# Another order of the work in the second layer of a four-layer graph network

## Chip, cores and metric

The kernel runs on one core of a Trainium2 chip. The metric is the device time of one execution in microseconds. Shares and durations below come from one further execution, recorded by the hardware profiler. Engine names are those of the profile: PE is the matmul engine, PEld its weight load, DVE the vector engine, ACT the scalar engine, POOL the GpSimd engine and SP the engine that issues most loads.

## What is computed

Input is `x`, 128 graphs of 64 nodes with 128 features, and `adj`, one 64 by 64 matrix of edge lengths for each graph. About a quarter of its entries are not zero. Four layers follow each other, each with a residual and a layernorm. Layers 0 and 1 are continuous-filter convolutions: every edge length is spread over Gaussians, two dense layers with a softplus make a filter of 128 numbers from it, and the filter weighs the neighbour's features. Layers 2 and 3 are graph convolutions with a normalised adjacency. Layer 1, with the constant log 2 left aside, and the chain of layers are:

```python
g  = jnp.exp(coeff * (e[:, :, :, None] - offsets) ** 2)
h  = ssp(jnp.einsum('bijg,fg->bijf', g, W1) + b1)
Wf = jnp.einsum('bijf,gf->bijg', h, W2) + b2
rf = jnp.einsum('bjd,fd->bjf', r, Wa)
y  = jnp.einsum('bjf,bijf->bif', rf, Wf * Am * Am)
y  = ssp(jnp.einsum('bif,df->bid', y, Wd1) + bd1)
y  = jnp.einsum('bid,ed->bie', y, Wd2) + bd2
...
x = _layernorm(x + _L1_gnn_ref(x, adj, adj, ...), axis=-1)
x = _layernorm(x + _L2_gnn_ref(x, adj, ...), axis=-1)
x = _layernorm(x + _L3_gnn_ref(x, adj, ...), axis=-1)
```

## The kernel before, in words

The kernel works only on the edges that are there. Two graphs form a pair; the 128 nodes of a pair are the 128 partitions. For each pair the edges are packed into slots, sorted so that all pairs of a set have the same number of slots, and the slots of a pair are cut into three chunks. There are 64 pairs and two filter layers, so the main loop of `sparse_stack` has 3 x 128 turns and two more; turn i works on pair n = i / 3 and chunk k = i mod 3. Turns with n from 64 on belong to layer 1.

A chunk goes through three turns. In its first turn `filter_in` (L1774) makes the first filter product px, and ACT takes the exponential and later the logarithm (`softplus`). In its second turn `gather` (L1800) makes pg, the neighbours' features by a product with a one-hot matrix, which ACT copies. In its third turn `filter_out` (L1788) makes the second filter product pw and `message` (L1814) on DVE adds the bias to pw and multiplies with the gathered features into m. px, pg and pw each have a single tile of two PSUM banks: the next px waits for the exponential, the next pg for the copy, and the next pw for the message. When a pair's third chunk is done, `slot_sums` (L1837, L1841) sums the messages of each node in eight pieces on DVE; the loop runs 1, 4 and 4 of these pieces in the turns k = 0, 1 and 2. With k = 0, DVE also makes the one-hot matrix of the pair (hot, L1762), and with k = 0 and 1 ACT makes the Gaussians of the next pair.

Beside this run three kinds of work on groups of pairs. All are Python generators that yield between two steps, and the function `slot` runs one step of a queue. A step that ends with products yields True, and what takes the result out of PSUM is issued in the next call of `slot`, whatever queue that is for. `node_before` (queue `befores`) transposes the features (xT) and makes the products y (L1453) that `gather` uses. `node_after` (queue `nodes`) makes the products u, o and back (L1565, L1584, L1593), adds the residual (ny, L1597) and normalises with `layernorm`. `graph_convs` (queues `convs`) makes layers 2 and 3 of the group: gx, gh, hw, nT, gh, hw, o, then a layernorm, then nT, sup, o, and a second layernorm, and hands the rows to `store_rows`, which scatters them to the output by DMAs that POOL issues. Convolutions of the groups follow in alternation in `convs[0]` and `convs[1]`. In `layernorm` the statistics are on DVE (L1415, L1416); for a group of four pairs the inverse root and the normalising of each pair are on POOL (L1422, L1423, L1428). `scaled` (L1630) puts the scaled adjacency into a block matrix on POOL.

Layer 1 begins with pair 8 and ends with pairs 0 to 7. It has groups of four pairs, and at its end groups of two, one and one, which have a queue of their own each in `last`. After the loop, all queues are drained in turn.

[...] a fixed order (`in_order`) is laid over all engines. So the order of the calls in the loop is the order of the products on PE. Before the change a turn's order on PE is px, pg, nodes, features (k = 1), the small groups, pw, convolutions.

## Time and profile before

| | |
|---|---|
| time, median of 3 runs | 1592.23 us (1591.06 to 1595.87) |
| profiled execution, time | 1607.39 us |
| profiled execution, span from first to last instruction | 1605.5 us |
| PE busy | 1432.6 us, 89% of the span |
| DVE, ACT, POOL busy | 1355.6, 1335.6, 732.5 us |
| share of PE in the chain that ended last | 45%, DVE 27%, ACT 10% |

The profiled execution is 15.2 us slower than the median. Layer 1 begins at about 760 us and its last pw starts at 1537.95 us. One group of four pairs takes twelve turns, for instance from 1235.60 to 1284.90 us. A line of the timeline has start, duration, engine, source line, operation, out<-in, shape and the number of equal instructions merged; in square brackets stands how long the engine had been idle and what released it. A line of the waits has the engine and what it wanted to do, whom it waited for, and then total, times and longest in us. The names of the products are those above; matmul rows count passes, so one product of two halves is x4.

### The profile page before, as it was taken

What the parts mean: (1) busy time and instruction counts of PE and PEld (TensorE: products, weight loads), DVE (VectorE), ACT (ScalarE), POOL (GpSimd) and SP (SyncE); (2) the same over time, 40 slices, a digit from 0 to 9 for tenths busy, and PEclk for the clock granted to TensorE, in tenths of its full rate; (3) what the DMA queues carried; (4) which work ended last, traced back from release to release, by engine and by line L of the source; (5) the groups of instructions that cost most, each with busy time, mean ns of one, the idle gap of its engine ahead of it and who ended that gap; (6) DMA issues with size and microseconds to landing.
All of it is one profiled execution on the core that took longest, in us unless ns stands there. A gap on an engine that the chain in (4) does not pass through costs nothing.

```text
span 1605.5 us, 24221 instructions
## 1 busy us (share of the span) xinstructions
PE 1432.6 (89%) x6813; PEld 802.6 (50%) x6813; DVE 1355.6 (84%) x3547; ACT 1335.6 (83%) x1847; POOL 732.5 (46%) x1174
## 2 busy tenths in 40 slices
PE   1276999999999999999999999999999999999974
PEld 1133454555554555555445555556555555555543
DVE  7687889999989999889878888888888888888873
ACT  1266898989888989889999998999989999899842
POOL 2425246555655644425611255433554435543454
PEclk9998999999999999999999999999999999999976
DMA  7654464645455544447555455544554455455200
GB/s 257 209 123 114 112 138 123 135 124 145 124 136 134 136 122 113 113 111 178 149 151 129 128 142 132 129 124 125 144 132 120 120 134 138 124 141 123 64 8 23
DMA packets 122289, 205.67 MB, mean 128 GB/s; under 512 B 47956, under 2 KB 80034, under 8 KB 121506
## 3 DMA queue, kind: packets, MB, share of 16 engines
q1 hardware_dynamic: 110784, 187.61, 46.7%
q0 software_dynamic: 6576, 14.99, 2.9%
q10 hardware_dynamic: 4786, 1.43, 0.4%
q8 instruction: 57, 0.93, 0.3%
q14 instruction: 86, 0.70, 0.2%
HBM read 185.29 MB, written 18.64 MB: 127 GB/s over the span
## 4 chain that ended last, share of the span: by engine, by line
PE 45%; DVE 27%; ACT 10%; DMA 7%; issue 6%; SPq 3%; POOL 2%; another core or an unknown queue 1%; ACTq 0%; DVEq 0%; POOLq 0%
PE pw L1788 16%; PE px L1774 9%; DVE m L1814 8%; PE pg L1800 7%; DVE agg L1837 6%; ACT h L951 4%; DVE hot L1762 2%; DVE at L1182 2%; PE hw L1673 2%; SPq L1299 2%; ACT g L951 2%; PE y L1453 2%; ACT d L951 1%; DVE st L1415 1%; PE o L1584 1%
## 5 line engine op out<-in xcount | busy, mean ns | idle before, releaser
L951 ACT ACTIVATE h<-h,half 128x672 f32<-128x672 f32 (+13 forms) x385 | 353.1, 917 | 0.1
L1837 DVE TENSOR_REDUCE agg<-m 128x16 f32<-128x240 f32 (+13 forms) x896 | 325.0, 411 | 3.0
L951 ACT ACTIVATE g<-pg 128x672 f32<-128x672 f32 (+12 forms) x384 | 303.2, 790 | 26.4 <-DVE m L1814 13.2
L1800 PE MATMUL pg<-hot,ys 64*128 64x336 f32 (+12 forms) x1536 | 308.8, 478 | 7.9 <-DVE hot L1762 7.0
L1788 PE MATMUL pw<-h,w_L_gnn_W2T 128*128 128x420 f32 (+5 forms) x768 | 301.9, 516 | 15.2 <-DVE m L1814 15.2
L1814 DVE SCALAR_TENSOR_TENSOR m<-pw,c_L_gnn_b,g 128x840 f32<-128x840 f32 (+5 forms) x192 | 200.9, 1046 | 115.6 <-PE pw L1788 88.0
L1788 PE MATMUL pw<-h,w_L_gnn_fw 128*128 128x336 f32 (+6 forms) x768 | 264.4, 467 | 28.3 <-DVE m L1814 22.0
L951 ACT ACTIVATE h<-px,c_L_gnn_b 128x840 f32<-128x840 f32 (+5 forms) x192 | 178.7, 931 | 53.6 <-PE px L1774 52.8
L1814 DVE SCALAR_TENSOR_TENSOR m<-pw,c_L_gnn_fb,g 128x672 f32<-128x672 f32 (+6 forms) x192 | 176.9, 921 | 50.0 <-PE pw L1788 31.2
L951 ACT ACTIVATE h<-px,c_L_gnn_fb 128x672 f32<-128x672 f32 (+6 forms) x192 | 159.3, 830 | 71.2 <-PE px L1774 46.4
L1788 PEld LDWEIGHTS pw<-h,w_L_gnn_W2T 128*128 128x128 f32 x768 | 132.5, 191 | 141.1 <-DVE m L1814 37.6
L1774 PE MATMUL px<-d,fw 64*128 64x336 f32 (+6 forms) x768 | 166.2, 507 | 40.8 <-DMA d<-d_dram 29.2
L1800 PEld LDWEIGHTS pg<-hot,ys 64*128 64x128 f32 x1536 | 146.3, 188 | 108.1 <-issue 17.5
L1788 PEld LDWEIGHTS pw<-h,w_L_gnn_fw 128*128 128x128 f32 x768 | 132.5, 191 | 120.6 <-DVE m L1814 62.2
L1762 DVE SCALAR_TENSOR_TENSOR hot<-j,row,w 128x1212 f32<-128x1212 bf16 (+12 forms) x128 | 177.0, 1383 | 9.0 <-issue 9.0
L1774 PE MATMUL px<-d,w1t 64*128 64x420 f32 (+5 forms) x768 | 181.1, 548 | 1.7 <-ACT h L951 1.6
L1422 POOL TENSOR_SCALAR rs<-mv 128x4 f32<-128x4 f32 x61 | 14.5, 237 | 344.0 <-DVE mv L1416 335.6
L1774 PEld LDWEIGHTS px<-d,fw 64*128 64x128 f32 x768 | 59.7, 188 | 132.2 <-ACT h L951 44.4
L951 ACT ACTIVATE d<-d,neg_off 128x1212 f32<-128x1212 f32 (+12 forms) x128 | 119.8, 936 | 7.1 <-issue 7.1
L1428 POOL TENSOR_SCALAR x_all<-ny,mv,rs 128x128 f32<-128x128 f32 x124 | 116.4, 947 | 3.3
L1030 POOL DMA_INDIRECT rows<-comb,goes x64 | 67.9, 1061 | 97.1 <-DMA rows<-comb,goes 69.6
L1774 PEld LDWEIGHTS px<-d,w1t 64*128 64x128 f32 x768 | 57.8, 184 | 66.8 <-ACT g L951 26.8
(264 smaller groups left out, 2209.6 us busy)
## 6 DMA issues: line engine op xcount, KB each, us to landing
d<-d_dram SPq DMA_DIRECT2D x32, 315.0 KB
w<-w_dram SPq DMA_DIRECT2D x32, 315.0 KB
d<-d_dram SPq DMA_DIRECT2D x32, 303.0 KB
w<-w_dram SPq DMA_DIRECT2D x32, 303.0 KB
w<-w_dram SPq DMA_DIRECT2D x32, 252.0 KB
j<-j_dram SPq DMA_DIRECT2D x32, 157.5 KB
j<-j_dram SPq DMA_DIRECT2D x32, 151.5 KB
d<-d_dram SPq DMA_DIRECT2D x16, 300.0 KB
```

Source lines behind the costliest of these rows:

```text
L951: latest = nc.scalar.activation(out_, in_, func, **kw)
L1030: nc.gpsimd.indirect_dma_start(out=into, out_offset=bass.IndirectOffsetOnAxis(ap=at, axis=0), in_=rows, in_offset=None,)
L1182: nc.vector.max_index(out=at[:, r, cut], in_max=top[:, r, cut], in_values=av[:, r, :])
L1299: (engine if name == "d" else nc.sync).dma_start(to, dram_ap(slots[layer, name][s], first, [[0, to.shape[0]], [1, n]]))
L1428: (nc.gpsimd if n == GS else nc.vector).tensor_scalar(dst[:, s, :], y[:, s, :], mv[:, s, 0:1], rstd[:, s : s + 1], ALU.subtract, ALU.mult,)
L1453: nc.tensor.matmul(ps[:, s, :], lhsT=xt[:, s * P : (s + 1) * P], rhs=w["win"], start=True, stop=True)
L1762: nc.vector.scalar_tensor_tensor(hots[n][:, 0:size], j[:, 0:size], near, wt[:, 0:size], ALU.is_equal, ALU.mult)
L1774: nc.tensor.matmul(ps[:, b, 0:n], lhsT=w1, rhs=d[rows, col : col + n], start=True, stop=True)
L1788: nc.tensor.matmul(c["pw"][:, b, :], lhsT=c["w"]["w2"], rhs=c["h"][:, b, :], start=True, stop=True)
L1800: nc.tensor.matmul(ps[:, b, 0:n], lhsT=y[rows, :], rhs=hots[c["n"]][rows, at], start=True, stop=True,)
L1814: nc.vector.scalar_tensor_tensor(messages[n][:, :, at], c["pw"], c["w"]["b2"], c["g"], ALU.add, ALU.mult)
L1837: nc.vector.tensor_reduce(av[:, :, :, r], both, AX.X, ALU.add)
```

## The change

Five edits, all of which act on layer 1 or on work that runs beside it.

1. In turns of layer 1, `filter_out` comes ahead of the small groups and the nodes' step. `message` stays behind them.
2. In turns of layer 1, the features' step runs with k = 0 instead of k = 1, right after `gather`.
3. `node_after` of layer 1 no longer yields once before u.
4. `graph_convs` of a group of four no longer waits two turns between the scaling and gx, and yields once more between sup and o.
5. The pieces of the sums run 2, 4 and 5 in the turns k = 0, 1 and 2 of layer 1.

```diff
         if layer == 0:
             yield from zero_share(q, agg)
-        elif q < len(GROUPS[1]) - 1:
-            yield
         u, _ = bank(f"u_{name}", n)
...
         if n == GS:
             scaled(2, q)
-            yield from wait_steps(2)
         flat, ps = bank(f"gx_{q}", n)
...
         y3 = yield from times("sup", lambda s: xs[:, s, :], lambda s: nT3[:, s, :])
+        if n == GS:
+            yield
         flat, ps = bank(f"o3_{q}", n)
...
-        run(sums, (1, 4, 4)[k])
+        run(sums, ((1, 4, 4), (2, 4, 5))[n >= NP][k])
...
         if c1 is not None:
             gather(c1)
+        if n >= NP and k == 0 and befores:
+            slot(befores)
         if c is not None:
             softplus(c)
             if k == 2 and sines:
 
                 sines.popleft()()
-        slot(nodes)
-        if k == 1 and befores:
-            slot(befores)
+        if n < NP:
+            slot(nodes)
+            if k == 1 and befores:
+                slot(befores)
+        if c2 is not None:
+            filter_out(c2)
         for queue in last.values():
             slot(queue)
+        if n >= NP:
+            slot(nodes)
         if c2 is not None:
-            filter_out(c2)
             message(c2)
         if convs[0]:
             slot(convs[0])
```

## Prediction

> **What bounds the kernel now.** I read the page's first part, then the busy table by stretches of time, then the waits of the matmul engine (PE) in layer 1, then one group of four pairs on each engine.

> ```profile
> PE 1432.6 (89%) x6813; PEld 802.6 (50%) x6813; DVE 1355.6 (84%) x3547; ACT 1335.6 (83%) x1847; POOL 732.5 (46%) x1174
> ```

> ```profile
> 850.00:1490.00 640.00, 621.21 (x3023) 356.24 (x3021) 535.49 (x1132) 590.00 (x748) 282.20 (x345) 1.00 0.52 131
> 1490.00:1606.00 116.00, 81.68 (x377) 53.39 (x376) 73.82 (x203) 59.01 (x116) 57.05 (x76) 0.82 0.09 24
> ```

> The columns of the second fence are stretch, length, busy PE, PEld, DVE, ACT, POOL, granted clock. The stretch 850 to 1490 is layer 1 with graph convolutions beside it: PE is busy 621.2 of 640 us, so an edit of order can win at most 18.8 us there. Then comes a tail of 116 us in which nothing is full. The waits of PE between 850 and 1490 say what the 18.8 us are:

> ```profile
> PE pw L1788 <- DVE m L1814: 15.2, 25, 1.1
> PE o L1584 <- ACT gy_hw L951: 1.6, 5, 0.3
> PE o L1726 <- ACT xt L951: 1.5, 1, 1.5
> PE px L1774 <- ACT h L951: 0.4, 1, 0.4
> ```

> 15.2 of 18.7 us are one wait: the second filter product pw (there is one pair of PSUM banks for it) cannot start before DVE's message m of the step before has read it. In the timeline it recurs in the same place of each group:

> ```profile
> 1273.61 1.56 PE L1788 MATMUL pw<-h,w_L_gnn_W2T 128*128 128x384 f32 x4
> 1275.09 0.92 PE L1774 MATMUL px<-d,w1t 64*128 64x384 f32 x4
> 1275.84 0.81 PE L1800 MATMUL pg<-hot,ys 64*128 64x384 f32 x4
> 1277.71 1.56 PE L1788 MATMUL pw<-h,w_L_gnn_W2T 128*128 128x384 f32 x4 [1.05 <-DVE m L1814]
> ```

> Between two pw stand only px and pg, 0.75 us each from start to start, and DVE has in that time the elu, reductions and layernorm statistics queued ahead of the message:

> ```profile
> 1274.03 0.74 DVE L1614 TENSOR_SCALAR er<-gh,c_L_gnn_b 128x512 f32<-128x512 f32 x1
> 1274.68 0.66 DVE L1837 TENSOR_REDUCE agg<-m 128x16 f32<-128x224 f32 x2
> 1275.26 0.67 DVE L1841 TENSOR_REDUCE agg<-m 128x8 f32<-128x256 f32 x2
> ...
> 1276.65 1.00 DVE L1814 SCALAR_TENSOR_TENSOR m<-pw,c_L_gnn_b,g 128x768 f32<-128x768 f32 x1
> ```

> So PE bounds layer 1, and its small bubbles come from uneven filling, not from a lack of DVE time: DVE is busy 535 of 640 us.

> [...] here the four normalising operations of one group take 3.1 us in some places and 3.87 us in others. I use that as the spread of their price.

> **Order of the products.** No arithmetic is added or removed, so I count what stands after each pw. For the group from 1235.60 to 1284.90 before: o; nothing; gx and y; gh and u; nT; sup; hw, o3 and o; nT and back; gh; nothing; nothing; hw and xT. In the changed program, same group: gx; gh; nT and y; sup; u and hw; nT and o3; gh; o; back; hw; o; xT. Three empty places become none, and the fullest holds two products instead of three. Prices from start to start in this group: pw 1.39 to 1.49, px and pg 1.50 together, a 128-column set of four 0.98, u or gh of 512 columns 0.96, a set of transposes 0.5. The sum over twelve steps is about 47.5 us in either order; before takes 49.30 with 1.66 idle. Placing a product after pw instead of before it moves 0.1 us (pw 1.39 against 1.29) from one to the other: cost nothing.

> **DVE in the new order.** Prices from start to start: message 0.95, hot 1.35, a reduction 0.38 (the last two 0.59), half the statistics of a layernorm 0.83, er, ny, gz, nT each 0.60, em with er 1.30. The sums' pace (2, 4, 5 in place of 1, 4, 4) costs no instruction: k=0 and k=2 steps get one reduction more, k=1 loses two. The heaviest stretch between two messages is the one after back: ny 0.6, er 0.6, two reductions 0.75, hot 1.35, statistics 0.83, message 0.95, together 5.1 us. A message ends at the earliest 2.6 us after its pw starts (1.5 + 0.1 + 1.0). 2.6 + 5.1 = 7.7 us stands against two PE periods of 3.9 = 7.8 us: no wait, but no room. All other stretches (2.1 to 4.9 us, against periods of 3.3 to 4.8) leave over 0.7 us. I take 0.3 us a group as what comes back, 0 to 0.7 as bounds; 13 groups: 4 us.

> **ACT.** Its heaviest step has h, g, softplus (2.3 us), u's three passes (1.9), the gaussian (1.05) and hw's copy (0.5), 5.7 us against a PE period of 4.8; the next ACT step has 2.9 against 4.5, and px needs only the exponential at its head. Cost nothing, hidden under pw and the step's two products; uncovered it would be 0.9 us a group.

> **Waiting turns removed.** Now gx follows back by four pw in place of seven: 15.0 us instead of 24.7. Between them lie the statistics and POOL's normalisation of x.

> ```profile
> 1280.16 0.23 POOL L1422 TENSOR_SCALAR rs<-mv 128x4 f32<-128x4 f32 x1 [0.74 <-DVE mv L1416]
> 1280.48 1.04 POOL L1423 TENSOR_TENSOR rs<-rs,neg_half 128x4 f32<-128x4 f32 x1
> 1281.62 3.87 POOL L1428 TENSOR_SCALAR x_all<-ny,mv,rs 128x128 f32<-128x128 f32 x4
> ```

> Before: back at 1268.84, x done at 1285.5, 16.7 us later, 8.0 us ahead of gx. After, ny is added one turn earlier, so x is due 13.2 to 13.8 us after back (7.7 to the last statistics, 0 to 0.6 behind a scatter and blocks, 5.5 on POOL): 1.2 to 1.8 us left. For sup the margin is thinner: POOL passes scatter, add, blocks, add, scatter (about 7.9 us with the waits for the scatter's DMA that the trace shows at 1.4 to 1.5 each), then 4.6 us of normalising: 26.0 us after back against sup at 26.6. When a scatter lands late (waits of up to 2.6 us are in the trace) PE stands at sup. Bounds 0 to 2 us a group, taken 0.4; 13 groups: 5 us. The bias add on xs and the scatters themselves are on POOL and are counted in this. SP's loads keep their order and turn. The features (xT, then y) go from the turn k=1 to k=0, one turn earlier; they are first gathered from in the next group, eight turns on, so nothing waits for them, and their copies on ACT (0.48 us each) are as many as before: cost nothing. Layer 0 keeps its order on all engines. The yield added after sup only places o3 one turn later, beside nT.

> **The tail.** After the last pw (1537.95) the end is 60 us away.

> ```profile
> 1547.51 1.06 PE L1685 MATMUL gx<-ident,x_all 128*128 128x128 f32 x4
> 1596.74 0.18 DVE L1416 BATCH_NORM_AGGREGATE mv<-st 128x2 f32<-128x6 f32 x1 [3.20 <-POOL gz L1428]
> ```

> This gx is that of the last convolution of four pairs; in the new order it stands ahead of the last pw, and 1.06 + 2.08 us of its products leave the stretch after u of the last pair. It also ends one turn earlier, so the last statistics need not wait 3.20 us for POOL's normalising of it. Against that, gx needs x (done at 1535.9), which can hold the last pw by 1 to 2 us, and the chain of the last pair keeps its turns. Gain between 0 and 6.3 us; I take 4.

> **Sum.** 18.7 - 4 - 5 + 4 = about 14 us, 15 with one px wait of 1.0 us at 818 that goes with the same spreading. The profiled execution would go from 1607.39 us (span 1605.5) to about 1592; its own 15 us over the median of 1592.23 is not part of this. Taken off the median: 1577.

> **Rivals.** All bubbles go and the tail gains in full: 18.7 + 6.3 = 25 us, 1567; for it speaks that no gap is empty; against it the 0.1 us of room after back. Half: the DVE wait reappears after back and hot at 0.7 us (9 us) with POOL's 5: 18.7 - 14 + 3 = 8 us, 1584. No difference: the tail is held by the last pair and the waits merely move; within 4 us of 1592. It would then not do what it says, though the order of the program is certain. Slower: POOL becomes the bound at sup and gx. From 1.75 us of wait a group on, (18.7 + 4) / 13, the change loses; with both scatter waits at 2.6 us and the normalising at 3.87, sup is late by about 2.6 us, which gives 13 x 2.6 - 22.7 = 11 us, 1603. For it speaks that POOL has waits on DMA in each group; against it, POOL is busy 282 of 640 us.

> **How the numbers follow.** Likeliest 1577 at 0.42, full 1567 at 0.20, half 1584 at 0.18, no difference 0.12, slower 0.08. Faster by over 0.3% (below 1587.5; about what a measurement of this kernel can tell from no change) is 0.80. The range 1566 to 1591 leaves out the slower case and the ends of the first and fourth.

> **What would show it.** Right: in the stretch of layer 1 PE's waits of pw for m fall from 15 us to under 5, the group's period is about 48 us, gx follows back by four pw, and the last wait of 3.2 us is gone. Wrong: PE waits for x_all of POOL at gx or sup by over 1 us a group, or the wait for m stays above 8 us, or the tail after the last pw stays at 60 us.

## Result and profile after

After 1580.67 us, median of 17 runs (1575.56 to 1590.36); before 1592.69 us, median of 17 runs (1589.88 to 1599.38). The ratio is 0.9915, 95% interval 0.990 to 0.993: the medians differ by 12.0 us, and the ratio alone gives 13.5, with 11 to 16 as its interval. The profiled execution after took 1590.36 us (span 1588.5); it is the slowest of the 17. That of before, with 1607.39 us, lies above all 17 of its runs too, so the traces are compared by stretches below.

First the profile's page, its busy times and the chain that ended last:

```profile
PE 1435.7 (90%) x6813; PEld 811.5 (51%) x6813; DVE 1358.1 (85%) x3547; ACT 1336.6 (84%) x1847; POOL 766.3 (48%) x1174
...
PE 34%; DVE 20%; DMA 14%; POOL 13%; ACT 9%; issue 6%; SPq 3%; ACTq 0%; DVEq 0%; POOLq 0%
```

The work is the same (equal counts of instructions). In the chain PE had 45% before, POOL 2% and DMA 7%; now POOL and DMA hold 27% together. The busy table by stretches:

```profile
850.00:1472.00 622.00, 614.00 (x2966) 357.48 (x2968) 527.10 (x1114) 575.80 (x729) 312.14 (x344) 0.99 0.51 131
1472.00:1589.00 117.00, 87.50 (x396) 56.47 (x394) 77.44 (x208) 65.90 (x123) 55.44 (x75) 0.82 0.13 34
```

PE's idle time in layer 1 fell from 18.8 us in 640 to 8.0 in 622. Its waits in that stretch are of another kind:

```profile
PE sup L1671 <- POOL x_all L1428: 5.6, 16, 0.8
PE gx L1682 <- POOL x_all L1428: 2.0, 3, 1.1
```

The wait of pw for DVE's message, 15.2 us before, is gone, and all that is left is a wait for POOL's normalising of x. In the group from xT at 1219.31 to xT at 1267.41 the period is 48.10 us, where it was 49.30.

I cut each execution in three: up to layer 1's first px (the first with `w1t`), from there to the start of the last pw (called layer 1 below), and the tail. Before: 745.00, 792.95, 67.55 us. After: 735.54, 788.22, 64.74 us. The first difference, 9.5 us, is no gain: nothing ahead of layer 1 was changed, and the profiled executions of all the kernels below begin layer 1 anywhere from 727.8 to 747.6 us. So this execution shows a gain of 7.5 us behind the start of layer 1; the other sixteen have no trace. What it lost lies in two groups, of 52.4 and 54.14 us. This is PE in the second:

```profile
1330.04 1.44 PE L1787 MATMUL pw<-h,w_L_gnn_W2T 128*128 128x380 f32 x4
1331.75 0.49 PE L1671 MATMUL sup<-nTs,x_all 128*128 128x128 f32 x2 [0.26 <-POOL x_all L1428]
1332.52 0.49 PE L1671 MATMUL sup<-nTs,x_all 128*128 128x128 f32 x2 [0.29 <-POOL x_all L1428]
1333.84 0.49 PE L1671 MATMUL sup<-nTs,x_all 128*128 128x128 f32 x2 [0.82 <-POOL x_all L1428]
1334.61 0.49 PE L1671 MATMUL sup<-nTs,x_all 128*128 128x128 f32 x2 [0.29 <-POOL x_all L1428]
1335.03 1.28 PE L1773 MATMUL px<-d,w1t 64*128 64x380 f32 x4
1336.09 1.48 PE L1799 MATMUL pg<-hot,ys 64*128 64x380 f32 x4
1337.51 2.19 PE L1787 MATMUL pw<-h,w_L_gnn_W2T 128*128 128x380 f32 x4
```

```profile
1325.00:1330.00 5.00, 5.00 (x30) 2.94 (x27) 5.00 (x12) 4.83 (x7) 4.39 (x6) 1.00 0.47 130
1330.00:1335.00 5.00, 3.34 (x14) 1.81 (x13) 3.21 (x5) 2.73 (x4) 4.56 (x4) 1.00 0.47 127
1335.00:1340.00 5.00, 5.00 (x15) 2.44 (x15) 0.19 (x1) 3.11 (x4) 0.00 (x0) 0.66 0.22 52
```

sup takes each pair of x as POOL finishes it, 0.49 us of work each 0.77 us or more. Right after it the granted clock (the share of PE's full clock that the chip allowed) is 0.66 over five microseconds, that is 3.4 us at half speed, and px, pg and pw take 1.28, 1.48 and 2.19 us where they took 0.91, 0.81 and 1.44 just before. PE had been busy for 2.01 us of the 3.41 ahead (last section). So PE lost more here than the length of the waits, but not behind all waits: three of 1.32 us in all at 1431 to 1433 were followed by a granted clock of 1.00.

### The profile page after: what moved, and what is told of

It is laid out like the page before. It is cut to its first block, busy times and chain, and to the rows that moved or that the text cites. A ratio compares the mean times of both kernels' runs of the same rounds, so it can differ in the third digit from the quotient of the medians.

```text
span 1588.5 us, 24203 instructions
## 1 busy us (share of the span) xinstructions
PE 1435.7 (90%) x6813; PEld 811.5 (51%) x6813; DVE 1358.1 (85%) x3547; ACT 1336.6 (84%) x1847; POOL 766.3 (48%) x1174
## 4 chain that ended last, share of the span: by engine, by line
PE 34%; DVE 20%; DMA 14%; POOL 13%; ACT 9%; issue 6%; SPq 3%; ACTq 0%; DVEq 0%; POOLq 0%
PE pw L1787 12%; PE px L1773 7%; PE pg L1799 5%; DVE m L1813 5%; POOL x_all L1428 5%; DMA out_dram<-gz,at_row 4%; ACT h L951 4%; DVE agg L1836 3%; DMA d<-d_dram 2%; DVE hot L1761 2%; POOL rs L1423 2%; SPq L1299 2%; POOL gz L1428 2%; DMA w<-w_dram 2%; ACT g L951 2%
## 5 line engine op out<-in xcount | busy, mean ns | idle before, releaser
L951 ACT ACTIVATE h<-h,half 128x672 f32<-128x672 f32 (+13 forms) x385 | 353.6, 918 | 0.1
L951 ACT ACTIVATE g<-pg 128x672 f32<-128x672 f32 (+12 forms) x384 | 303.4, 790 | 30.2 <-DVE m L1813 18.3
L1836 DVE TENSOR_REDUCE agg<-m 128x16 f32<-128x240 f32 (+13 forms) x896 | 319.5, 411 | 2.9
L1787 PE MATMUL pw<-h,w_L_gnn_W2T 128*128 128x420 f32 (+5 forms) x768 | 306.9, 522 | 1.3 <-DVE m L1813 1.2
L951 ACT ACTIVATE h<-px,c_L_gnn_fb 128x672 f32<-128x672 f32 (+6 forms) x192 | 159.3, 830 | 55.9 <-PE px L1773 55.6
L951 ACT ACTIVATE h<-px,c_L_gnn_b 128x840 f32<-128x840 f32 (+5 forms) x192 | 178.7, 931 | 27.0 <-PE px L1773 26.3
L1422 POOL TENSOR_SCALAR rs<-mv 128x4 f32<-128x4 f32 x61 | 14.7, 241 | 310.5 <-DVE mv L1416 308.5
L951 ACT ACTIVATE d<-d,neg_off 128x1212 f32<-128x1212 f32 (+12 forms) x128 | 120.3, 940 | 6.7 <-DMA d<-d_dram 6.7
L1030 POOL DMA_INDIRECT rows<-comb,goes x64 | 70.8, 1106 | 94.6 <-DMA rows<-comb,goes 60.4
L1428 POOL TENSOR_SCALAR x_all<-ny,mv,rs 128x128 f32<-128x128 f32 x124 | 106.2, 864 | 3.3
```

Source lines behind the costliest of these rows:

```text
L951: latest = nc.scalar.activation(out_, in_, func, **kw)
L1030: nc.gpsimd.indirect_dma_start(out=into, out_offset=bass.IndirectOffsetOnAxis(ap=at, axis=0), in_=rows, in_offset=None,)
L1422: nc.gpsimd.tensor_scalar(rstd, mv[:, :, 1], LN_EPS, None, ALU.add)
L1428: (nc.gpsimd if n == GS else nc.vector).tensor_scalar(dst[:, s, :], y[:, s, :], mv[:, s, 0:1], rstd[:, s : s + 1], ALU.subtract, ALU.mult,)
L1787: nc.tensor.matmul(c["pw"][:, b, :], lhsT=c["w"]["w2"], rhs=c["h"][:, b, :], start=True, stop=True)
L1836: nc.vector.tensor_reduce(av[:, :, :, r], both, AX.X, ALU.add)
```

## Experiments

My theory was that places between two pw that hold no other product make the wait for the message, and that filling them removes it. The rivals: DVE's backlog of reductions makes it; and POOL, pressed by the removed turns, is the next bound. "Layer 1" is the length defined above, of the profiled execution; 792.95 us before, 788.2 after. The waits of PE are those from 850 us on.

### Each edit alone

Edit 1 alone (`filter_out` ahead of the nodes' step):

```diff
-        slot(nodes)
+        if n < NP:
+            slot(nodes)
...
+        if c2 is not None:
+            filter_out(c2)
         for queue in last.values():
             slot(queue)
+        if n >= NP:
+            slot(nodes)
         if c2 is not None:
-            filter_out(c2)
             message(c2)
```

> The kernel before with edit 1 alone: pw ahead of the nodes' step in layer 1. Theory of the filled places (the gain is that no two pw of layer 1 stand without a product between them while DVE is behind): this order still has two empty places next to each other in each group, so PE's wait for m stays at 10 to 15 us between 850 us and the end of layer 1, and the time is within 4 us of 1592.7. Rival, pw early (the gain is that pw starts earlier): most of it shows here, about 1582 us.

Edit 2 alone (the features' step with k = 0):

```diff
+        if n >= NP and k == 0 and befores:
+            slot(befores)
...
-        if k == 1 and befores:
+        if n < NP and k == 1 and befores:
             slot(befores)
```

> The kernel before with edit 2 alone: xT and y with k = 0 instead of k = 1. The order of the products has one empty place in a group instead of three. Theory of the filled places: PE's wait for m falls by about half, 1585 to 1588 us. Rival, pw early: no change, within 3 us of 1592.7.

Edits 3 and 4 alone (the turns of waiting):

```diff
-        elif q < len(GROUPS[1]) - 1:
-            yield
...
-            yield from wait_steps(2)
...
+        if n == GS:
+            yield
```

> The kernel before with edits 3 and 4 alone: no waiting turns in the nodes and convolutions, one turn between sup and o. Two empty places in a group, not next to each other. Theory of the filled places: wait for m about half, and the tail about 3 us shorter: 1583 to 1588 us; PE may wait for POOL's x_all at gx or sup by 1 to 3 us in all. Rival, the tail alone is the gain: 1588 us with the wait for m unchanged at 15 us.

Edit 5 alone (the pace of the sums):

```diff
-        run(sums, (1, 4, 4)[k])
+        run(sums, ((1, 4, 4), (2, 4, 5))[n >= NP][k])
```

> The kernel before with edit 5 alone: the sums run 2, 4, 5 instead of 1, 4, 4. Order on PE as before. Theory of the filled places: within 3 us of 1592.7, wait for m 12 to 17 us. Rival, the gain is an even load of DVE: 1583 us with the wait for m under 7 us.

| alone | us (median) | ratio to before, 95% | layer 1 | PE waits in layer 1 |
|---|---|---|---|---|
| edit 1 | 1589.83 | 0.9987 (0.9972 to 1.0002) | 789.3 | pw for m 8.5, o for ACT's copy of sup 3.5 |
| edit 2 | 1589.39 | 0.9979 (0.9966 to 0.9991) | 787.6 | pw for m 11.9 |
| edits 3 and 4 | 1652.04 | 1.0368 (1.0342 to 1.0395) | 852.8 | below |
| edit 5 | 1593.85 | 1.0009 (0.9998 to 1.0021) | 792.4 | pw for m 15.3 |

The medians of edits 1 and 2 are 2 to 3 us lower, but the interval of edit 1 includes no change; edit 5 wins nothing. With edit 2 the wait for m fell by a fifth, where I had expected half, and with edit 1 it fell below the 10 to 15 us that I had expected. Edits 3 and 4 alone lose 59 us, where I had expected a gain. Their waits of PE:

```profile
PE gx L1682 <- POOL x_all L1428: 22.4, 32, 1.4
PE sup L1671 <- POOL x_all L1428: 17.0, 30, 2.5
```

The wait for m is gone there too, but 39.4 us of waiting for POOL came instead, and 44.4 us of layer 1 run at half clock (before: 3.4 us, at its very end); the mean granted clock of the whole execution is 0.970, before 0.982. PE idles 25.7 us more than before in layer 1 and is busy for 34.1 us longer. Of the latter the half clock is at most 20.5 us by estimate, half of the 41.0 us that it lasts longer; the other 13.6 may be gx and sup, which come there in single pieces; that was not tried. So the rival "POOL becomes the bound" is real.

### Which half needs which

The changed kernel with the turns of waiting put back, that is edits 1, 2 and 5:

```diff
+        elif q < len(GROUPS[1]) - 1:
+            yield
...
+            yield from wait_steps(2)
...
-        if n == GS:
-            yield
```

> The changed kernel with the turns of waiting back (edits 1, 2 and 5 alone). Theory of filled places: one place between two pw stays empty in a group, and POOL has its room, so no wait of PE for x_all and no half-clock stretch; some 5 us of pw waiting for m stay: 1580 to 1586. Theory that the removed turns are what hurts (as in the run with edits 3 and 4 alone, +59 us): without them the time is below that of the changed kernel, 1572 to 1578. Rival: that edits 1 and 2 together already fill what matters and the turns are free in this company: the time of the changed kernel, within 3 us.

1630.17 us, ratio 1.0238 (1.0209 to 1.0268), layer 1 821.4 us. All three expectations failed. pw waits 0.2 us for m, so edits 1 and 2 do fill the places; but sup waits 19.5 us in 41 pieces for POOL. Neither half of the change is of use alone, and both lose to the same engine. POOL in that kernel, one group:

```profile
1279.98 1.58 POOL L1449 TENSOR_TENSOR x_all<-x_all,b_L_gnn_bd 128x512 f32<-128x512 f32 x1 [1.44 <-PE xT L1444]
...
1287.41 1.10 POOL L1030 DMA_INDIRECT out_dram<-gz,at_row  x1 [0.18 <-issue]
1288.54 0.62 POOL L1630 TENSOR_TENSOR blocks<-a_all,dinv 64x256 f32<-64x256 f32 x1
1292.29 2.61 POOL L1630 TENSOR_TENSOR blocks<-a_all,dinv 64x256 f32<-64x256 f32 x3 [3.13 <-DMA out_dram<-gz,at_row]
1295.18 1.00 POOL L1030 DMA_INDIRECT out_dram<-gz,at_row  x1 [0.28 <-POOL blocks L1630]
1300.23 0.96 POOL L1030 DMA_INDIRECT out_dram<-gz,at_row  x1 [4.05 <-DMA out_dram<-gz,at_row]
```

In this trace the second block scaling behind a scatter, or the next scatter, waits until it has landed: 4.9 us from 1287.41 to 1292.29, 5.05 from 1295.18 to 1300.23. After, the same stretch is:

```profile
1268.76 2.08 POOL L1030 DMA_INDIRECT out_dram<-gz,at_row  x1 [0.18 <-issue]
1270.88 1.28 POOL L1449 TENSOR_TENSOR x_all<-x_all,b_L_gnn_bd 128x512 f32<-128x512 f32 x1
1272.10 0.62 POOL L1628 TENSOR_TENSOR blocks<-a_all,dinv 64x256 f32<-64x256 f32 x1
1273.19 0.61 POOL L1628 TENSOR_TENSOR blocks<-a_all,dinv 64x256 f32<-64x256 f32 x1 [0.47 <-DMA out_dram<-gz,at_row]
1273.88 1.28 POOL L1686 TENSOR_TENSOR x_all<-x_all,b_L_gnn_b 128x512 f32<-128x512 f32 x1
...
1277.85 4.00 POOL L1428 TENSOR_SCALAR x_all<-gz,mv,rs 128x128 f32<-128x128 f32 x4
```

The add L1449 (1.28 us) stands between a scatter and what waits for it, and the wait is 0.47 us. That gave a new theory: what makes x late is how the scatters lie in POOL's queue.

### Is DVE the cause of the old wait, and is the pace needed

The kernel before with layer 1's sums over two slots instead of all for seven of eight residues; it leaves out part of the messages:

```diff
-            one = v[:, :, base[r] : base[r] + caps[r]]
+            one = v[:, :, base[r] : base[r] + (2 if layer == 1 else caps[r])]
```

> The kernel before with layer 1's sums of messages taken over two slots instead of all for seven of eight residues: it leaves out part of the messages, so that DVE's reductions are shorter and their number the same. Theory that PE's waits of pw for m come from empty places in PE's own order (a wait of the length of the message's chain minus the work between): the waits fall in part, as far as reductions stand ahead of the message, to some 8 to 12 us, time 1580 to 1588. Rival, they come from DVE's backlog of reductions: the waits fall below 4 us and the time to 1576 to 1580.

1580.14 us, ratio 0.9909 (0.9887 to 0.9931), layer 1 778.5 us. The wait of pw for m:

```profile
PE pw L1788 <- DVE m L1814: 4.5, 11, 0.5
```

That is nearer to the rival. DVE's reductions ahead of the message make it late: with shorter ones, in PE's old order, 10.7 of the 15.2 us go. Filled places give DVE time, shorter reductions need less.

The changed kernel with the pace of before, `run(sums, (1, 4, 4)[k])`:

> The changed kernel with the sums' old pace (1, 4, 4) in layer 1. Theory that the pace is of no weight, as alone: within 2 us of the changed kernel. Rival, the pace is needed in the new order (four reductions ahead of the message in the turn k=1, in which hot and the products' results now come too): pw waits for m again by 4 us or more, and the time is 4 to 8 us above the changed kernel.

1581.56 us, ratio 0.9918 (0.9894 to 0.9943), layer 1 781.9 us, no wait for m. The pace is of no weight in the new order either. This execution had one half-clock stretch, behind four waits of gx (2.6 us); its mean granted clock is 0.988.

### Where POOL's lateness comes from

First try: the changed kernel with the second block scalings early.

```diff
+            scaled(3, q)
             yield
         else:
             nT = normals[2, q]
...
-        if n == GS:
-            scaled(3, q)
         yield True
         z = by_pair(tiled("gz2", n, q))
```

> The changed kernel with the second pair of block scalings on POOL issued after the first normalised matrix is read, some turns earlier, in a stretch in which POOL idles, so that they and the wait for the scatter's DMA no longer stand ahead of the statistics and of the normalising of x. Theory that POOL's lateness at gx and sup costs the waits (7.6 us) and, through the half-clock stretches after them, some 9 us more in two groups: both go, 1568 to 1574, and a narrower spread of executions. Rival, the scalings aren't what makes x late (the normalising itself and the scatters are): waits of PE for x_all stay at 5 us or more, and the time within 3 us of the changed kernel.

1583.67 us, ratio 0.9928 (0.9899 to 0.9957): no gain over the changed kernel. Layer 1 takes 783.0 us and has no half-clock stretch, but 4.2 us of waits for x_all stay, and pg waits 3.6 us for DVE. The landing only found another to wait: scatters wait 37.6 us for the scatter ahead of them.

So I took out the scatters of the first groups (all that end at pair 52 or lower; their rows of the output are not written), in the changed kernel and in both halves.

```diff
-        else:
+        elif pairs.stop > NP - 3 * GS:
             stores.append(store_rows(pairs, z))
```

> The changed kernel with the scatters of the first twelve or so groups of layer 1 left out (their rows of the output are not written), so that neither a scatter nor an operation that waits for a scatter's DMA stands ahead of the statistics and the normalising of x on POOL. Theory that POOL is late at gx and sup because of the scatters and their landing: no wait of PE for x_all, no half-clock stretch before the tail, 1570 to 1577, spread of the executions under 8 us. Rival, the normalising itself and its slower repeats beside DVE make x late: waits for x_all of 3 us or more stay and the time is within 3 us of the changed kernel (1578 to 1584).

> The kernel with edits 3 and 4 alone (1652), with the same scatters left out (their rows of the output are not written). Theory that its +59 us are POOL's waits for scatters to land (56 us of waits of POOL in its trace), passed on to PE at gx and sup and multiplied by half-clock stretches: both waits of PE go, 1576 to 1588. Rival, gx is late for want of turns between the layernorm and gx, whatever POOL does: gx waits of some 20 us stay, 1615 to 1640.

> The kernel with edits 1, 2 and 5 alone (1630), with the same scatters left out (their rows of the output are not written). Theory that its +37 us are POOL's waits for scatters to land: the waits of PE at sup (19.5 us in 41 pieces) go, 1572 to 1584. Rival, POOL's add of the features, which waits for xT ahead of the statistics there, makes the chain late by itself: waits at sup of over 8 us stay, 1600 to 1625.

Beside these three runs the kernel before took 1611.29 us (1604.85 to 1618.97), 18 us more than beside the others, so only ratios and layer 1 compare; their traces begin layer 1 late, at 745.7 to 747.6 us, so part of the 18 us probably lies ahead of it:

| | with scatters | without | layer 1, with and without |
|---|---|---|---|
| changed kernel | 0.9915 (0.990 to 0.993) | 0.9875 (0.9849 to 0.9902) | 788.2, 776.0 |
| edits 3 and 4 | 1.0368 (1.0342 to 1.0395) | 0.9936 (0.9912 to 0.9959) | 852.8, 784.3 |
| edits 1, 2 and 5 | 1.0238 (1.0209 to 1.0268) | 0.9926 (0.9902 to 0.9950) | 821.4, 784.0 |

No wait of PE for x_all is left in any of the three, and both losses turn into gains of about 0.7%. Taken off 1592.69 the ratios are 1573, 1582 and 1581 us, each where the theory had it. The waits of PE that the two halves keep are, with edits 3 and 4 alone,

```profile
PE u L1563 <- DVE agg L1840: 8.9, 14, 1.5
```

and with edits 1, 2 and 5

```profile
PE o L1731 <- ACT gy_sup L951: 3.5, 6, 0.7
```

The scatters in POOL's queue are shown to be the cause of both losses. The rival of the last run, the add L1449 that waits for xT ahead of the statistics, is not a cause by itself: without scatters it waits 70.8 us, with them 52.9. How much is the landing, and how much the issue of a scatter (about 1 us each), these runs do not separate; the last run below, which still issues them all, speaks for the landing. That the kernel before would not gain from their absence was not tried; its PE waits for POOL nowhere in layer 1.

Last, all the work, with the scatters in other steps:

```diff
-        run(stores, 1)
+        if i % 2 or i % 12 == 4 or i >= 3 * (N - 2 * GS):
+            run(stores, 1)
```

> The changed kernel with all its work, and the four scatters of a group in four steps that are chosen: each stands behind the block scalings of its step and two of them behind the normalising of x for sup, so that no operation of POOL waits for a scatter that has just been issued. Theory that the landing of scatters in POOL's queue is what makes x late: no waits of PE for x_all, no half-clock stretch in layer 1, and the gain of the run without scatters: a ratio to the kernel before of 0.985 to 0.990, that is 1569 to 1577 where before takes 1593. Rival, the scatters issued later hold the buffer of their rows longer, and DVE's copy of the next normalised matrix, with the messages behind it, waits for the last of them: waits of PE for DVE of 5 us or more, and the ratio of the changed kernel (0.990 to 0.993) or worse.

1580.21 us (1575.48 to 1581.63, 6 runs), ratio 0.9913 (0.9891 to 0.9936). One group on POOL:

```profile
1254.67 3.13 POOL L1428 TENSOR_SCALAR x_all<-ny,mv,rs 128x128 f32<-128x128 f32 x4
...
1264.68 1.11 POOL L1030 DMA_INDIRECT out_dram<-gz,at_row  x1 [0.16 <-issue]
1265.84 0.25 POOL L1422 TENSOR_SCALAR rs<-mv 128x4 f32<-128x4 f32 x1
1266.17 1.05 POOL L1423 TENSOR_TENSOR rs<-rs,neg_half 128x4 f32<-128x4 f32 x1
1267.33 3.13 POOL L1428 TENSOR_SCALAR x_all<-gz,mv,rs 128x128 f32<-128x128 f32 x4
1270.63 1.10 POOL L1030 DMA_INDIRECT out_dram<-gz,at_row  x1 [0.18 <-issue]
1273.31 0.96 POOL L1030 DMA_INDIRECT out_dram<-gz,at_row  x1 [1.57 <-DMA out_dram<-gz,at_row]
```

No wait for a landing stands ahead of either normalising. PE is then full:

```profile
850.00:1455.00 605.00, 603.52 (x2947) 351.46 (x2945) 530.86 (x1108) 571.30 (x724) 304.85 (x344) 1.00 0.51 133
```

The mechanism is as expected: PE idles 1.5 us in 605, the clock stays at 1.00, layer 1 takes 775.7 us, 17.3 less than before. The time is not: the ratio is that of the changed kernel, with a narrower range of runs (6 us against 15, but of fewer runs). In the profiled execution the tail takes 68.6 us against 64.74 after: 1.5 us come from an hw and the two products behind it at half clock (hw at 1519.96 takes 2.93 us for 12 pieces, where 8 take 1.05 elsewhere), and 2.4 us lie behind the last DVE instruction, where the last rows land. Whether other executions give back the same is open. There is a simpler reading: the trace after is that of its slowest execution, and the fastest one of the changed kernel, 1575.56 us, equals the fastest here, 1575.48. Most executions of the changed kernel may lack the disturbed groups that this edit removes; they were not traced.

## Why the prediction was right, step by step

The predicted 1577 stands against 1580.67. Its working against what was measured:

- **Order of the products: right.** pw no longer waits for m; from 884 us on, groups of four pairs that nothing disturbs are 0.8 to 1.8 us shorter; and the period of 48.10 us is the forecast 48. My reason, uneven filling "not from a lack of DVE time", was half of it: shorter reductions alone won as much (0.9909).
- **DVE in the new order, taken at 4 us: 0.** The message behind the heaviest stretch, after back (1254.22), ends at 1260.33, 0.2 us ahead of the pw that needs it; I had left 0.1 us:

```profile
1259.33 1.00 DVE L1813 SCALAR_TENSOR_TENSOR m<-pw,c_L_gnn_b,g 128x768 f32<-128x768 f32 x1
```

```profile
1260.56 1.56 PE L1787 MATMUL pw<-h,w_L_gnn_W2T 128*128 128x384 f32 x4
```

- **ACT at nothing: right in the whole**, but for a reason that I had not named. The yield after sup, which I put down as only placing o one turn later, removes o's wait for ACT's copy of sup: 3.5 us wherever edit 1 stands without it (edit 1 alone, and edits 1, 2 and 5 without scatters).
- **Turns removed, taken at 5 us: mis-sized, 7.6 us of waits in the profiled execution.** gx follows back by 14.97 us (15.0 forecast) and x is done after 14.36, where I had 13.2 to 13.8: 0.6 us are left, not 1.2 to 1.8. sup follows by 26.5 (26.6), x is done after 27.6 where I had 26.0. Two terms were too small. Behind the last statistics (done at 1261.72) POOL turns to the roots for gx only at 1263.98, 2.3 us later, held by a block scaling that waits for a scatter, where I had 0 to 0.6; the roots and normalising then took 4.6, where I had 5.5. And the normalising for sup with its roots, for which I had 4.6 us, took 5.5 in this group (from 1276.37) and 6.2 in the disturbed one, beside DVE's hot. The half-clock stretches behind such waits were not in the sum at all.
- **Features at nothing: right for edit 2 alone and in the whole, but not in all company.** I followed xT's and y's copies on ACT and left out the add L1449 on POOL, which waits for xT. With edits 1, 2 and 5 it stands ahead of the statistics and no longer fills the landing that the block scaling waits for, and that kernel loses 37 us; without scatters it loses nothing. In the full change it does fill a landing, so that there it cost nothing, by luck.
- **Sums' pace at nothing: right**, alone and in the new order.
- **Tail, taken at 4 us: 2.8.** I had put the end 60 us behind the last pw; that is where DVE ends (1597.87), and the span ends 67.55 behind it. The last wait of 3.20 us became 1.84 and did not vanish, and sup now waits 2.10 us for POOL. The px wait of 1.0 us near 818 became 0.6.
- **The slower rival: the right mechanism at too low a price.** Edits 3 and 4 alone have 39.4 us of PE waits for POOL, 3.0 us for each of 13 groups, and lose 59 us, where the rival's own sum would have given 39.4 - 22.7 = 17. At most 20.5 us of the difference are the half clock, by the estimate above; the rest is open. With the whole change POOL just keeps up.

The sum: 18.7 - 0 - 7.6 + 2.8 = 13.9 us; the profiled execution shows 7.5. Its two disturbed groups are 9.9 us longer than their neighbours, and the waits in them make 4.6 of that. Each has 3.4 us at half clock, which by estimate cost half of that, 1.7, so 3.4 in both; the last 1.9 fit sup, whose four pieces of 0.49 us stand where eight products in a row take 1.05 (with the scatters in other steps). Neither was in the sum, and with both 1.1 us stay open. An error of 4 us on DVE's side and errors on POOL's side offset each other.

## What to carry to other kernels

Before turns of waiting are taken out, write down for each engine in the chain what stands in its queue between the two ends, with the landings it waits for; here a helper engine at 46% busy was the next bound. Edits that share a queue have no separate worth: here two halves that lose 2.4% and 3.7% make a gain of 0.85%. Compare stretches inside the trace when the start of an execution moves by more than the effect.

## What the hardware showed

```profile
1332.02:1335.43 3.41, 2.01 (x10) 1.22 (x11) 1.77 (x4) 1.00 (x2) 2.54 (x3) 1.00 0.81 214
1335.43:1338.84 3.41, 3.41 (x10) 1.53 (x7) 0.00 (x0) 2.42 (x4) 0.00 (x0) 0.50 0.21 48
```

With scalings early, divided at 1333.86 in the third wait, PE is busy for 2.44 and 2.72 us of two stretches of that length:

```profile
1330.45:1333.86 3.41, 2.44 (x10) 1.19 (x8) 2.83 (x4) 2.71 (x4) 3.31 (x4) 1.00 0.22 70
1333.86:1337.27 3.41, 2.72 (x13) 1.58 (x14) 0.36 (x2) 1.45 (x3) 1.13 (x2) 1.00 0.79 192
```

Busy time alone does not decide. Ahead of the three stretches at half clock in layer 1 of the traces before and after stands a step with PE busy for 1.46 us (before), 2.33 and 2.01 us (after), but seven other steps at full clock with 1.95 to 2.38 us were followed by none, among them that of 1457.81 before, with 1.95, and that of 1431.00 after, with 2.20. What decides was not shown.
- **POOL's normalising beside DVE.** Four normalising operations take 3.12 to 3.13 us beside reductions, messages and statistics, and 3.85 to 4.96 us beside hot: in the timelines of before, between 850 and 1475 us, all 12 that took over 3.4 us overlap hot (L1762) by 1.4 us or more, and none of the 23 shorter ones does. After, 11 of 11 over 3.8 us overlap hot by 1.2 us or more, and another 11, of 3.21 to 3.68 us, overlap er (L1618) and ny (L1595) by 0.68 us or more each; none of the 15 at 3.12 to 3.13 us overlaps these two, and 12 of them overlap a message by 1.0 us or more. Why hot, er and ny go with the longer times and the message does not was not shown; no run separates it.
- **The landing of a scatter.** What waits for it goes on 2.7 us (scatters in other steps, 1270.63 to 1273.31) to 5.05 us behind its issue in the stretches quoted here; where the trace after notes a landing, it comes 2.2 to 5.8 us behind, with a median of 4.1. Between 850 and 1472 us after, block scalings on POOL wait 29.1 us in all for landings, in 20 waits, and before, between 850 and 1490, the next scatter goes on 2.5 to 2.6 us behind the one ahead of it, at the end of such a wait. What stands between does not wait itself: with the scatters in other steps the roots start 1.16 and the normalising 2.65 us behind the scatter of 1264.68, and after, the add starts 2.12 us behind that of 1268.76, which took 2.08 us to issue.
